# A second modulation in two halves, and seven smaller moves between VectorE, ScalarE and GpSimd, in a two-layer transformer kernel

## The chip, the cores and the metric

The kernel runs on one core of one Trainium2 chip, in one launch. The metric is the device time of one execution in microseconds (us). Three executions of the kernel before gave a median of 621.16 us (621.09 to 622.55).

A core has five engines that take part here. TensorE multiplies matrices and transposes, VectorE, ScalarE and GpSimd do elementwise work, and SyncE (SP) mostly issues DMA transfers. Each engine takes its instructions strictly in its own order. An instruction whose input is not there yet holds all that stand behind it on its engine.

## The reference, cut to what matters

Two layers run one after the other over `x` of 8 batches, 256 tokens and 128 features. In each layer a small vector `c` per batch is turned into six modulation vectors, which scale, shift and gate the two halves of the layer. The change touches layer 0 and the modulation of layer 1.

```python
mod = (silu(c) @ wmod).reshape(8, 6, 1, 128)       # once for each layer
sa, ca, ga, sb, cb, gb = mod[:, 0], ..., mod[:, 5]
ga = (2 * (ga >= 0) - 1) * maximum(abs(ga), 0.25)  # gb likewise
h = layernorm(x) * (1 + ca) + sa
x = x + ga * attention(h)
h = layernorm(x) * (1 + cb) + sb
x = x + gb * mixture(h)

# layer 0, attention: 16 heads of 8 features, causal
qkv = x @ W_qkv + b_qkv
scores = einsum('bhqd,bhkd->bhqk', q, k) / sqrt(8)  # then the causal mask
out = softmax(scores) @ v, heads put together
return out @ W_out + b_out
# layer 0, mixture: a shared network 128 -> 512 -> 128 (gelu), and of
# eight experts of the same size the two best of each token
probs = softmax(x @ Wr); topk_p, topk_i = top_k(probs, 2)
```

Layer 1 has 16 heads of 64 features and sixteen small experts, again two for each token.

## The kernel before, in words

**Two paths.** `fast_path` does all the work. It leaves out the subtraction of the maximum in the softmax, so it keeps a record of whether the row sums stayed in a safe range: `judge` (L798) folds reciprocals of row sums into a tile `good` with two VectorE steps (L801, L802). At the end a flag says whether `general_path` has to run as well. With these inputs it does not.

**The order of work.** The functions called in `fast_path` issue instructions at once, so the order of calls is the order in which each engine gets its instructions. A hand-written plan sets it. Lists `at`, `at_end` and `at_head` attach small steps to the passes of one loop, and the loop is this (L1421):

```python
for n in range(N0):          # N0 = 24 passes: 8 batches of 3 units
    b, u = divmod(n, 3)
    scores0(b, u, ...)       # 4 matmuls, 2 exps, masks; at_head steps inside
    if n == 0: set_up()
    if u == 1 and b + 1 < B: project0(b + 1)
    ...                      # the steps given by at(n, ...)
    if n > 1: values0(*divmod(n - 2, 3))
    if u == 1 and b + 1 < B: project_v0(b + 1)
    ...                      # the steps given by at_end(n, ...)
```

**A unit** is one pass. Units 0 and 1 of a batch take the first 128 keys for half of the heads each, unit 2 takes the last 128 keys and queries. `scores0` fills two score tiles `sc` in PSUM with two matmuls each (L1095), ScalarE takes an exp of 128x1024 from each into `pt` (L1099), and GpSimd clears what the causal mask forbids (L806). `values0` for the unit two passes back multiplies `pt` with the values into `o` (L1120). The values tile `vm` holds, for each head, 8 columns of values in a field of 32, with a column of ones at 16 or 17, which gives the row sum.

**Projections of a batch.** In the middle unit of a batch `project0` makes queries and keys of the next one: two matmuls `qk` (L1059), the key bias by one VectorE step (L1062), and four copies `qm` of the queries by ScalarE, each with the heads of one group kept and biased (L1064). `project_v0` comes at the end of the same unit: two matmuls `vp` and eight VectorE steps that add the value bias and place the columns into `vm` (L1081).

**After a batch.** At the end of the next batch's middle unit, `normalise0` (L1126) turns `o` around (`ot`), takes the reciprocals `r` of the row sums, scales (`at`) and turns back (`aT`). Two units later `finish0` (L1150) projects `aT` (`y`, L1156), scales by the gate `ga` and adds to `x`; `judge0` then tests the batch's reciprocals. The output bias, already multiplied by the gate, is added to `x` for two batches at a time by `add_bias`, a 128x512 addition on GpSimd (L1148).

**Norms.** `layernorm_parts` (L730) splits a norm into `measure` (statistics `st`, mean and variance `mv`), `normalise` (reciprocal root `rstd`, then `xn`, L756) and `modulate` (transposes `nt`, L765, and `h`, L768). For the tags listed in `by_power` the reciprocal root is made by two GpSimd steps at the end of `measure`: an addition (L745) and a power (L746). For all other norms ScalarE takes a root (L752) and VectorE a reciprocal (L753) in `normalise`. The first-half norms of layer 0 are `0a0` to `0a3`, for two batches each. The second-half norms are `0b0`, `0b2`, `0b4` for two batches and `0b6`, `0b7` for one. `0b2` and `0b4` are measured in units 15 and 21, `0b6` and `0b7` after the loop. [...] a change between the root, the exp (L1099, and L1200 in the router) and the gelu (L1233) loads a table.

**The router** of layer 0 (`route0`, L1185) follows each second-half norm: logits `lg`, an exp, the best two of eight, the slot of each token, and then one indirect DMA for each 128 tokens and choice (L910), which GpSimd issues and which writes the normalised tokens (`tokens`, two GpSimd steps) sorted by expert into DRAM. The steps are given out one at a time, over units 10 to 14 and the following heads, 16 to 20, and 22 to the end. After the loop (L1438 to L1492) come the last batches, the shared network (`shared_hidden0`, L1230), and a range test `judge0` of the last batch. Then 39 expert tiles of 128 tokens run (L1495): rows come by DMA, `turn0` transposes them (`xT`, `xTs`), `hidden0` and `tile_project0` apply the expert, a copy `ysb` of the result goes to DRAM. Copies `ysb` take two buffers in turn, those of the tags `aT` and `r`. Each buffer of a pool is reused only after its last reader is done.

**Modulation.** `modulation(n)` (L674) makes six projections `mp` on TensorE (L677; a matmul counts twice in the trace[...]) and moves them into `md[n]` with three VectorE steps (L681 to L683). `finish_modulation(n)` (L685) does twelve more tiny VectorE steps: one plus `cb`, the clamped gates, and the gated bias (L697). `rows_of(n, md)` (L699) transposes the result (`mr`, L702), copies it and sends it to DRAM, from where layer 1 will read it as rows. For layer 1 the three are called one behind the other at the end of unit 2, by `second_modulation`.

Of the kernel before, what the change touches and what calls it, by code (L numbers as in the profile page):

```python
# [16 lines left out]
P = 128  # L17
# [5 lines left out]
H = 16  # L23
# [534 lines left out]
def fast_path(ctx: ExitStack, tc: tile.TileContext, i: dict, out: bass.AP, bad: bass.AP):  # L558
# [62 lines left out]
    for base, cm, step in ((0, 1, -D0), (D0 - 1, -1, D0)):  # L621
# [1 line left out]
            out=hm, in_=hm, compare_op=ALU.is_ge, fill=0.0, base=base,  # L623
            pattern=[[step, H]], channel_multiplier=cm,
        )
    vm = [ap0.tile([P, 2, H, 32], F32, tag=f"vm{n}", bufs=1, name=f"vm{n}") for n in range(3)]

    def clear_vm(n):
        nc.gpsimd.memset(vm[n], 0.0)
        for m in range(2):  # L630
            nc.gpsimd.memset(vm[n].rearrange("p k (a m) c -> p (k a) m c", m=2)[:, :, m, 16 + m : 17 + m], 1.0)

    clear_vm(0)
    ints = const.tile([P, 65], I32, name="ints")
# [95 lines left out]
    def layernorm_parts(w, m, ks, kc, tag, ps_, tokens=None, tiles=range(TT)):  # L730

        kept = []
        nt = len(tiles)
        by_power = tag.startswith(('0a', '0b0', '1a0'))

        def measure():
            st = small.tile([P, nt, 6], F32, tag="st", name=f"st{tag}")
            mv = small.tile([P, nt, 2], F32, tag="mv", name=f"mv{tag}")
            for k, j in enumerate(tiles):
                nc.vector.bn_stats(st[:, k, :], x[w][:, j, :])  # L740
            for k in range(nt):
                nc.vector.bn_aggr(mv[:, k, :], st[:, k, :])
            rstd = small.tile([P, nt, 1], F32, tag="rstd", name=f"rstd{tag}")
            if by_power:
                nc.gpsimd.tensor_tensor(rstd, mv[:, :, 1:2], eps.unsqueeze(1).to_broadcast([P, nt, 1]), ALU.add)  # L745
                nc.gpsimd.tensor_tensor(rstd, rstd, minus_half.unsqueeze(1).to_broadcast([P, nt, 1]), ALU.pow)  # L746
            kept.extend((mv, rstd))

        def normalise():
            rstd, mv = kept.pop(), kept.pop()  # L750
            if not by_power:
                nc.scalar.activation(rstd, mv[:, :, 1:2], AF.Sqrt, bias=eps)  # L752
                nc.vector.reciprocal(rstd, rstd)  # L753
            xn = lnp.tile([P, nt, P], F32, tag="xn", name=f"xn{tag}")
            for k, j in enumerate(tiles):
                nc.vector.tensor_scalar(  # L756
                    xn[:, k, :], x[w][:, j, :], mv[:, k, 0:1], rstd[:, k, :], ALU.subtract, ALU.mult
                )
            kept.append(xn)

        def modulate():
            xn = kept[0]
            nt_ps = ps_([P, nt * P], f"nt{tag}")
            for k in range(nt):
                nc.tensor.transpose(nt_ps[:, bass.ts(k, P)], xn[:, k, :], ident)  # L765
            for k in range(nt * P // S):
                b = w * (TW // S) + tiles[0] * P // S + k
                nc.vector.tensor_scalar(  # L768
                    batch_cols(h, b), nt_ps[:, bass.ts(k, S)], m[:, kc, b : b + 1], m[:, ks, b : b + 1],
                    ALU.mult, ALU.add,  # L770
                )
            if tokens:
                tokens(w, xn)

        return [measure, normalise, modulate]
# [279 lines left out]
    def project0(b):  # L1055
        hb = batch_cols(h, b)
        qk = ps_ln([P, 2, S], f"qk0_{b}")
        for k in range(2):
            nc.tensor.matmul(out=qk[:, k, :], lhsT=wqkv[:, bass.ts(k, P)], rhs=hb, start=True, stop=True)  # L1059
        qm = ap0.tile([P, 4, S], F32, tag="qm", name=f"qm0_{b}")  # L1060
        k = ap0.tile([P, S], F32, tag="k", name=f"k0_{b}")
        nc.vector.tensor_scalar(k, qk[:, 1, :], bqkv[:, 1:2], None, ALU.add)  # L1062
        for j in range(4):
            nc.scalar.activation(  # L1064
                qm[:, j, :], qk[:, 0, :], AF.Identity, bias=jb[:, j : j + 1], scale=jm[:, j : j + 1]
            )
        st0["qk", b] = qm, k

    def project_v0(b):
        hb = batch_cols(h, b)  # L1070
        vp = ps_ln([P, 2, P], f"vp0_{b}")
# [4 lines left out]
        v = vm[b % 3].rearrange("p k (g j) m -> p (k g) j m", j=4)  # L1076
        vs = vp.rearrange("p k (g j d) -> p (k g) j d", j=4, d=D0)
        bs = bv.rearrange("p (g j d) -> p g j d", j=4, d=D0)
        for j in range(4):
            for n in range(2):  # L1080
                nc.vector.tensor_tensor(  # L1081
                    v[:, bass.ts(n, 4), j, bass.ts(j % 2, D0)], vs[:, bass.ts(n, 4), j, :], bs[:, :, j, :], ALU.add
                )

    def scores0(b, u, between):

# [22 lines left out]
    def values0(b, u):  # L1109
        v = vm[b % 3]  # L1110
        pt = st0.pop(("pt", b, u))
        if u == 0:
            st0["o", b] = pp.tile([P, 2, S], F32, tag="o", name=f"o0_{b}")
        o = st0["o", b]

        for n in range(2 if u < 2 else 4):
            j = 2 * u + n if u < 2 else n
            for g in range(4):
                q = bass.ds(0, S) if u < 2 else bass.ds(P, P)
                nc.tensor.matmul(  # L1120
                    out=o[bass.ts(g, 32), j // 2, q], lhsT=v[:, u // 2, 4 * g + j, :],
                    rhs=pt[:, g, bass.ts(n, S if u < 2 else P)],
                    start=(u == 0 and n == 0), stop=(u == 2 and n == 3), skip_group_check=True,
                )

    def normalise0(b):  # L1126

        o = st0.pop(("o", b))
        ot = ap0.tile([P, 2, S // 32, 32], F32, tag="ot", bufs=1, name=f"ot0_{b}")
        nc.vector.transpose(ot.rearrange("p s k c -> p (s k c)"), o.rearrange("p s q -> p (s q)"))  # L1130
        r = st0["r", b] = ap0.tile([P, 2, S // 32, 2], F32, tag="r", name=f"r0_{b}")
        nc.vector.reciprocal(r, ot[:, :, :, 16:18])
        at = ap0.tile([P, S // 32, 2, 2, D0], F32, tag="t", name=f"at0_{b}")
        for s in range(2):
            nc.vector.tensor_tensor(
                at[:, :, s], ot[:, s, :, 0:16].rearrange("p k (m d) -> p k m d", m=2),
                r[:, s].unsqueeze(3).to_broadcast([P, S // 32, 2, D0]), ALU.mult,
            )
        aT = ap0.tile([P, S], F32, tag="aT", name=f"aT0_{b}")
        nc.vector.transpose(aT, at.rearrange("p k s m d -> p (k s m d)"))  # L1140
        st0["aT", b] = aT

    def judge0(b):
        judge(st0.pop(("r", b)).rearrange("p s k m -> p (s k m)"))

    def add_bias(w):

        nc.gpsimd.tensor_tensor(by_batch(x[w]), by_batch(x[w]), of_batches(mdb0[:, BG - 1], w), ALU.add)  # L1148

    def finish0(b):  # L1150
        aT = st0.pop(("aT", b))
# [148 lines left out]
    def tile_project0(n):  # L1300
        hs, wt = tl.pop(("hs", n)), tl.pop(("w", n))
        y = pp.tile([P, P], F32, tag="o", name=f"yt_{n}")
        for c in range(FC):
            nc.tensor.matmul(  # L1304
                out=y, lhsT=hs[:, c, :], rhs=wt[:, bass.ds(WF + c * P, P)], start=(c == 0), stop=(c == FC - 1)
            )
        ysb = ap0.tile([P, P], F32, tag=("aT", "r")[n % 2], name=f"ysb_{n}")
        nc.vector.tensor_copy(ysb, y)  # L1308
        nc.sync.dma_start(out=z0.ys[bass.ts(n, P), :], in_=ysb)

# [36 lines left out]
        nc.gpsimd.memset(most, P - 0.5)  # L1347

    N0 = 3 * B
    at_head(2, 0, lambda: add_bias(0))  # L1350
    at_end(2, lambda: second_modulation())
    for w in range(1, NW):
        measure, normalise, modulate = layernorm_parts(w, md[0], SA, CA, f"0a{w}", ps_ln)
        n = 6 * w - 6
        at_end(n, measure)
        at(n + 1, normalise)
        at_end(n + 3, modulate)
        at_head(n + 2, 1, lambda w=w: add_bias(w))
    for b in range(B - 1):
        at_end(3 * b + 4, lambda b=b: normalise0(b))  # L1360
        if b < B - 2:
            at(3 * b + 6, lambda b=b: finish0(b))
            at_end(3 * b + 6, lambda b=b: judge0(b))
        else:
            at_end(3 * b + 5, lambda b=b: finish0(b), lambda b=b: judge0(b))
    ways = {}
    for bs in SPANS0[:3]:
        n = 3 * sum(bs) + 3
# [23 lines left out]
    z0 = Sorted(xp, "0", E0, NTT, (2 * NT - 2) // P)  # L1392
    z1 = Sorted(xp, "1", E1, 3 * TT, ND1)
    gates = ap0.tile([P, NTT, 32], F32, bufs=1, name="gates")
    wst = []

    def set_up():
# [15 lines left out]

    rd1 = []

    def second_modulation():
        modulation(1)
        finish_modulation(1)
        rd1.append(rows_of(1, md[1]))

    for n in range(N0):  # L1421
        b, u = divmod(n, 3)
        scores0(b, u, behind.pop(n, {}))
# [1 line left out]
            set_up()  # L1425
        if u == 1 and b + 1 < B:
            project0(b + 1)
        for step in early.pop(n, ()):
            step()
        if n > 1:  # L1430
            values0(*divmod(n - 2, 3))
        if u == 1 and b + 1 < B:
            project_v0(b + 1)
        for step in ends.pop(n, ()):
            step()

# [49 lines left out]
    for n in range(E0, E0 + 2):  # L1486
        fetch_weights0(n)
    one(shared_add0(1))()
    judge0(B - 1)
    turn_gates0(3)  # L1490
    shared_project0(2)
    tables()  # L1492
# [725 lines left out]
```

## Time and profile before

The lines that matter, from the profile of one execution:

| | |
|---|---|
| median of three executions | 621.16 us (621.09 to 622.55) |
| the profiled execution | 625.56 us; span 623.8 us, mean granted clock 0.940 |
| busy in the span: TensorE matmuls, weight loads | 548.0 us (88%), 388.9 us (62%) |
| VectorE, ScalarE, GpSimd | 352.9 us (57%), 275.8 us (44%), 292.0 us (47%) |
| chain of waits, by engine | TensorE 63%, VectorE 18%, DMA 8%, ScalarE 4% |
| layer 0's attention loop | from about 16 to 134 us |
| expert tiles of layer 0 | from 170 to 253 us, one every 1.89 us |
| layer 1 | from about 265 us |

The span runs from the first to the last instruction in the trace; the device time includes a little around it. All times within the execution are counted from the start of the span. "PE" is TensorE's matmul pipe and "PEld" its weight loads, "DVE" is VectorE, "ACT" ScalarE, "POOL" GpSimd. The page cuts the span into 40 slices of equal length and gives each engine's busy share in tenths for each slice, and for "PEclk" the clock that TensorE was granted. A wait is printed as the waiting instruction, an arrow, and the instruction that released it. An instruction is printed with its output, its inputs, the tiles' shapes and a count.

### The profile page before, as it was taken

To read this page: it belongs to the slowest core of one execution; us is meant where nothing else is said; L and a number is where in the kernel's file an instruction comes from. 1 tells how busy PE (TensorE), PEld (TensorE's weight loads), DVE (VectorE), ACT (ScalarE), POOL (GpSimd) and SP (SyncE) were. 2 spreads that over 40 slices of the span, in tenths; PEclk is the share of its full clock that TensorE was granted. 3 is DMA by queue.
4 is the path that set the end of the run, shared out by engine and by line. 5 is a ranking of instruction groups with operands and counts; after the bars stand their busy time and mean duration, and the time that the engine had idled before them with its cause. 6 is when DMAs were issued, how large, how long until landed. Compare 5 with 4: busy or idle time off the path is not lost.

```text
span 623.8 us, 11930 instructions
## 1 busy us (share of the span) xinstructions
PE 548.0 (88%) x4391; PEld 388.9 (62%) x4391; DVE 352.9 (57%) x1073; ACT 275.8 (44%) x487; POOL 292.0 (47%) x445
## 2 busy tenths in 40 slices
PE   5698979878799998789999999999999998988970
PEld 3344435445699998656676767667676766764450
DVE  5538896855732221246536556565838485644683
ACT  2566565545055554345534363345353532522430
POOL 5536686866314442238532056643445543104750
PEclk9989888879999998979999999999999999878986
DMA  7799991220329997131030203130303036563441
GB/s 271 281 399 407 393 362 52 65 90 30 108 71 325 316 333 231 35 151 35 19 86 6 64 18 88 30 73 2 78 14 82 18 74 187 165 176 76 105 104 57
DMA packets 53568, 85.41 MB, mean 137 GB/s; under 512 B 6653, under 2 KB 32765, under 8 KB 52349
## 3 DMA queue, kind: packets, MB, share of 16 engines
q1 hardware_dynamic: 45308, 60.50, 30.7%
q0 software_dynamic: 8048, 23.67, 12.3%
q8 instruction: 37, 0.61, 0.4%
q10 hardware_dynamic: 144, 0.39, 0.2%
q14 instruction: 31, 0.25, 0.1%
HBM read 53.46 MB, written 31.07 MB: 136 GB/s over the span
## 4 chain that ended last, share of the span: by engine, by line
PE 63%; DVE 18%; DMA 8%; ACT 4%; issue 3%; POOL 2%; SPq 1%; DVEq 0%; POOLq 0%; ACTq 0%
PE sc L1581 7%; PE o L1603 6%; PE qp L1550 5%; PE hp L1296 5%; PE vp L1563 5%; PE kp L1550 4%; PE yt L1304 4%; PE y L1656 4%; DMA wt<-in_wpk_dram,widx 3%; PE sc L1095 3%; PE sum L1611 3%; PE o L1120 2%; PE qk L1059 2%; PE hp L1230 1%; DMA gp<-gd 1%
## 5 line engine op out<-in xcount | busy, mean ns | idle before, releaser
L806 POOL TENSOR_SCALAR_AFFINE_SELECT pt<-pt 128x256 f32<-128x256 f32 (+1 forms) x176 | 89.4, 533 | 112.1 <-ACT pt L1584 79.8
L1033 POOL DMA_INDIRECT yg<-ys,yidx x56 | 54.1, 966 | 52.8 <-DMA ys<-ysb 34.5
L1584 ACT ACTIVATE pt<-sc 128x768 f32<-128x768 f32 x64 | 48.5, 808 | 25.6 <-PE sc L1581 25.4
L1099 ACT ACTIVATE pt<-sc 128x1024 f32<-128x1024 f32 x48 | 46.5, 1021 | 24.0 <-PE sc L1095 23.0
L1025 POOL DMA_INDIRECT wt<-in_wpk_dram,widx x31 | 29.1, 938 | 52.8 <-PE xT L1287 51.1
L1298 ACT ACTIVATE hst<-hp,wt 128x128 f32<-128x128 f32 x136 | 38.9, 368 | 32.9 <-ACT hst L1298 18.8
L1581 PEld LDWEIGHTS sc<-q,k 64*128 64x128 f32 x512 | 41.5, 187 | 16.5 <-issue 11.5
L1581 PE MATMUL sc<-q,k 64*128 64x256 f32 (+1 forms) x512 | 50.5, 336 | 0.0
L1603 PE MATMUL o<-pt,v 128*64 128x256 f32 (+1 forms) x512 | 48.7, 332 | 1.8 <-POOL pt L806 1.8
L1566 ACT COPY v<-vp 128x512 f32<-128x512 f32 x32 | 18.8, 586 | 67.9 <-PE vp L1563 57.1
L1308 DVE COPY ysb<-yt 128x128 f32<-128x128 f32 x39 | 11.4, 292 | 60.6 <-PE yt L1304 60.6
L1603 PEld LDWEIGHTS o<-pt,v 128*64 128x64 f32 x512 | 31.9, 136 | 19.7 <-POOL pt L806 5.6
L1554 DVE COPY q<-qp 128x512 f32<-128x512 f32 x32 | 22.0, 688 | 39.0 <-PE qp L1550 39.0
L1095 PE MATMUL sc<-qm,k 32*128 32x512 f32 x192 | 37.7, 738 | 3.4 <-ACT pt L1099 2.7
L1296 PE MATMUL hp<-xTs,wt 128*128 128x128 f32 x272 | 37.4, 281 | 3.7 <-DMA wt<-in_wpk_dram,widx 2.7
L1550 PE MATMUL qp<-h,wq 128*128 128x256 f32 x128 | 37.0, 412 | 1.3 <-DVE sh L1257 1.3
L910 POOL DMA_INDIRECT xs<-ht0b,idx x32 | 31.7, 990 | 13.4 <-issue 4.8
L1563 PE MATMUL vp<-wv,h 128*128 128x512 f32 x64 | 36.4, 652 | 1.1 <-DVE q L1554 1.1
L1296 PEld LDWEIGHTS hp<-xTs,wt 128*128 128x128 f32 x272 | 33.8, 195 | 5.5 <-issue 3.3
L1304 PE MATMUL yt<-wt,hst 128*128 128x128 f32 x272 | 36.6, 279 | 0.0
L1554 ACT COPY k<-kp 128x512 f32<-128x512 f32 x32 | 18.8, 588 | 35.4 <-PE kp L1550 35.4
L1304 PEld LDWEIGHTS yt<-wt,hst 128*128 128x128 f32 x272 | 33.9, 196 | 0.0
(289 smaller groups left out, 1129.8 us busy)
## 6 DMA issues: line engine op xcount, KB each, us to landing
xs<-zero SPq DMA_DIRECT2D x1, 12288.0 KB
xs<-zero SPq DMA_DIRECT2D x1, 8192.0 KB
rb<-rd SPq DMA_DIRECT2D x14, 512.0 KB
mdb<-mrd SPq DMA_DIRECT2D x2, 2048.0 KB
xg<-xs SPq DMA_DIRECT2D x63, 64.0 KB
wt<-in_wpk_dram SPq DMA_DIRECT2D x24, 128.0 KB
wst<-in_wpk_dram SPq DMA_DIRECT2D x5, 514.0 KB
ys<-ysb SPq DMA_DIRECT2D x10, 256.0 KB
```

What stands on the lines that cost most here:

```text
L806: nc.gpsimd.affine_select(out=pt, in_=pt, compare_op=ALU.is_ge, fill=0.0, base=0, pattern=[[0, pt.shape[1]], [1, P]], channel_multiplier=-1,)
L1033: nc.gpsimd.indirect_dma_start(out=yg[:, k, :], out_offset=None, in_=self.ys[:, :], in_offset=bass.IndirectOffsetOnAxis(ap=self.yidx[:, j, ...
L1095: nc.tensor.matmul(out=sc[:, n, :].rearrange("p (a q) -> p a q", q=rhs.shape[2]), lhsT=k[r, cols], rhs=rhs, start=True, stop=True,)
L1099: nc.scalar.activation(pt[:, bass.ts(half, 2), :], sc, AF.Exp)
L1296: nc.tensor.matmul(out=hp[:, c, :], lhsT=wt[:, bass.ts(c, P)], rhs=xT, start=True, stop=True)
L1304: nc.tensor.matmul(out=y, lhsT=hs[:, c, :], rhs=wt[:, bass.ds(WF + c * P, P)], start=(c == 0), stop=(c == FC - 1))
L1550: nc.tensor.matmul(out=ps_[:, n, :], lhsT=w1[f"w{what}1"][:, bass.ts(2 * u + n, P)], rhs=hb, start=True, stop=True)
L1554: copy(st1[what, b, u], ps_)
L1563: nc.tensor.matmul(out=vp, lhsT=hb[:, bass.ts(j, P)], rhs=w1["wv1"][:, bass.ts(half, 512)], start=True, stop=True)
L1581: nc.tensor.matmul(out=sc[:, n, cols], lhsT=k[r, m, bass.ts(kb, P)], rhs=q[r, m, qs], start=True, stop=True)
L1584: nc.scalar.activation(pt, sc[:, :, 0:384], AF.Exp, scale=1.0 / math.sqrt(D1))
L1603: nc.tensor.matmul(out=o[bass.ts(n, D1), m, qs], lhsT=v[:, kb, bass.ts(4 * (u % 2) + 2 * m + n, D1)], rhs=pts[m][:, n, cols], start=(kb == ...
```

## The change

Seven things are changed.

- The three parts of the second modulation are called at three places: the projections at the end of unit 3, the small VectorE steps at the end of unit 4, the transposition and its DMA at the end of unit 7.
- All norms of layer 0 take the reciprocal root by GpSimd's power; no ScalarE root is left in layer 0.
- The key bias is added by ScalarE, ahead of the four query steps, not by VectorE.
- The value bias of a batch is one VectorE step. For that, the ones of `vm` lie at columns 16 and 41 of a field of 64 for each pair of heads, and the odd head's window of 32 columns begins at 24.
- The bias on `x` is added by VectorE, at the ends of units 3, 8, 14 and 20; before, GpSimd did it at heads of units 2, 2, 8 and 14.
- The reciprocals of all batches are kept in one tile `rs0` and tested once, ahead of the expert tiles, by two steps over 256 elements a partition.
- `project_v0` is called right behind `project0`.

As a consequence `r` is no tag of the pool any more, and the copies `ysb` take the tags `aT`, with two buffers, and `ot`, with one.

```diff
-    vm = [ap0.tile([P, 2, H, 32], F32, ...) for n in range(3)]
+    vm = [ap0.tile([P, 2, H // 2, 64], F32, ...) for n in range(3)]
...
-            nc.gpsimd.memset(vm[n]...[:, :, m, 16 + m : 17 + m], 1.0)
+            nc.gpsimd.memset(vm[n]...[:, :, 16 + 25 * m : 17 + 25 * m], 1.0)
...
-        by_power = tag.startswith(('0a', '0b0', '1a0'))
+        by_power = tag.startswith(('0', '1a0'))
...
-        nc.vector.tensor_scalar(k, qk[:, 1, :], bqkv[:, 1:2], None, ALU.add)
+        nc.scalar.activation(k, qk[:, 1, :], AF.Identity, bias=bqkv[:, 1:2])
...
-        for j in range(4):
-            for n in range(2):
-                nc.vector.tensor_tensor(
-                    v[:, bass.ts(n, 4), j, bass.ts(j % 2, D0)], vs[:, bass.ts(n, 4), j, :], bs[:, :, j, :], ALU.add
-                )
+        nc.vector.tensor_tensor(
+            vm[b % 3].rearrange("p k a (m c) -> p k (a m) c", m=2)[:, :, :, 0:D0],
+            vp.rearrange("p k (h d) -> p k h d", d=D0),
+            bv.rearrange("p (h d) -> p h d", d=D0).unsqueeze(1).to_broadcast([P, 2, H, D0]), ALU.add,
+        )
...
-                    out=o[bass.ts(g, 32), j // 2, q], lhsT=v[:, u // 2, 4 * g + j, :],
+                    out=o[bass.ts(g, 32), j // 2, q], lhsT=v[:, u // 2, 2 * g + j // 2, bass.ds(24 * (j % 2), 32)],
...
-        r = st0["r", b] = ap0.tile([P, 2, S // 32, 2], F32, tag="r", name=f"r0_{b}")
+        r = rs0[:, b]
...
-    def judge0(b):
-        judge(st0.pop(("r", b)).rearrange("p s k m -> p (s k m)"))
...
-        nc.gpsimd.tensor_tensor(by_batch(x[w]), by_batch(x[w]), of_batches(mdb0[:, BG - 1], w), ALU.add)
+        nc.vector.tensor_tensor(by_batch(x[w]), by_batch(x[w]), of_batches(mdb0[:, BG - 1], w), ALU.add)
...
-        ysb = ap0.tile([P, P], F32, tag=("aT", "r")[n % 2], name=f"ysb_{n}")
+        tag, bufs = (("aT", 2), ("ot", 1))[n % 2]
+        ysb = ap0.tile([P, P], F32, tag=tag, bufs=bufs, name=f"ysb_{n}")
...
-    at_head(2, 0, lambda: add_bias(0))
-    at_end(2, lambda: second_modulation())
+    at_end(3, lambda: add_bias(0), lambda: modulation(1))
+    at_end(4, lambda: finish_modulation(1))
+    at_end(7, lambda: rd1.append(rows_of(1, md[1])))
...
-        at_head(n + 2, 1, lambda w=w: add_bias(w))
+        at_end(n + 8, lambda w=w: add_bias(w))
...
-            at_end(3 * b + 6, lambda b=b: judge0(b))
...
-            at_end(3 * b + 5, lambda b=b: finish0(b), lambda b=b: judge0(b))
+            at_end(3 * b + 5, lambda b=b: finish0(b))
...
+    rs0 = ap0.tile([P, B, 2, S // 32, 2], F32, bufs=1, name="rs0")
...
             project0(b + 1)
+            project_v0(b + 1)
...
-        if u == 1 and b + 1 < B:
-            project_v0(b + 1)
...
-    judge0(B - 1)
+    judge(rs0.rearrange("p b s k m -> p (b s k m)"))
```

More of the change, by code (lines that the diff above doesn't have):

```diff
@@ L625, in fast_path @@
         )
-    vm = [ap0.tile([P, 2, H, 32], F32, tag=f"vm{n}", bufs=1, name=f"vm{n}") for n in range(3)]
+    vm = [ap0.tile([P, 2, H // 2, 64], F32, tag=f"vm{n}", bufs=1, name=f"vm{n}") for n in range(3)]
     def clear_vm(n):
@@ L630, in clear_vm @@
         for m in range(2):
-            nc.gpsimd.memset(vm[n].rearrange("p k (a m) c -> p (k a) m c", m=2)[:, :, m, 16 + m : 17 + m], 1.0)
+            nc.gpsimd.memset(vm[n].rearrange("p k a c -> p (k a) c")[:, :, 16 + 25 * m : 17 + 25 * m], 1.0)
     clear_vm(0)
@@ L1075, in project_v0 @@
             )
-        v = vm[b % 3].rearrange("p k (g j) m -> p (k g) j m", j=4)
-        vs = vp.rearrange("p k (g j d) -> p (k g) j d", j=4, d=D0)
-        bs = bv.rearrange("p (g j d) -> p g j d", j=4, d=D0)
-        for j in range(4):
-            for n in range(2):
-                nc.vector.tensor_tensor(
-                    v[:, bass.ts(n, 4), j, bass.ts(j % 2, D0)], vs[:, bass.ts(n, 4), j, :], bs[:, :, j, :], ALU.add
-                )
+        nc.vector.tensor_tensor(
[3 more added lines that the diff above has]
+        )
     def scores0(b, u, between):
@@ L1414, in fast_path @@
     rd1 = []
[L1416 to L1419, printed above, removed]
     for n in range(N0):
```

## The prediction

> **What bounds the kernel now.** I read the page's slices, then TensorE's waits inside the attention loop of layer 0, then the chain, then timelines of the spots these name. The slices (15.6 us each) place the edits: all but the `ysb` buffers lie in the first eleven, and layer 1, from about 265 us, runs the same instructions as before.
>
> ```profile
> PE   5698979878799998789999999999999998988970
> DVE  5538896855732221246536556565838485644683
> POOL 5536686866314442238532056643445543104750
> PEclk9989888879999998979999999999999999878986
> ```
>
> TensorE is nearly full from slice 10 on. In slices 1 to 9 it has gaps, and VectorE and GpSimd stand at 8 and 9 there. No engine is full alone: they hand a wait to each other. The waits of TensorE from 22 to 134 us (total us, times, longest):
>
> ```profile
> PE mr L702 <- DVE md L697: 5.2, 1, 5.2
> PE nt0b L765 <- DVE xn0b L756: 4.2, 4, 2.5
> PE qk L1059 <- DVE h L768: 3.9, 2, 3.6
> PE sc L1095 <- ACT pt L1099: 1.8, 5, 1.2
> PE y L1156 <- DVE aT L1140: 1.3, 2, 0.8
> ```
>
> The first is the second modulation: its transposition `mr` stands in TensorE's queue behind fifteen small VectorE steps, and everything after it waits. The chain of waits shows the same (start, us, what):
>
> ```profile
> 25.45 1.45 PE mp L677 x12
> ...
> 31.84 0.15 DVE md L697
> ...
> 32.13 0.38 PE mr L702
> 32.51 2.02 PE sc L1095 x8
> 34.53 1.86 PE o L1120 x16
> ```
>
> The same eight score matmuls take 1.07 us at 37.21 and sixteen value matmuls 1.00 at 24.45, so the wait also costs half speed afterwards. The third view is unit 21 to 22 (a unit is one pass of the loop, a third of a batch), where a norm of the second half of layer 0 runs:
>
> ```profile
> 115.97 0.35 DVE L742 BATCH_NORM_AGGREGATE mv0b<-st0b 128x2 f32<-128x6 f32 x4
> 116.36 0.30 ACT L752 ACTIVATE rstd0b<-mv0b,eps 128x4 f32<-128x4 f32 x1 [1.48 <-DVE mv0b L742]
> 117.07 1.35 DVE L756 TENSOR_SCALAR xn0b<-x,mv0b,rstd0b 128x128 f32<-128x128 f32 x4
> ```
>
> ```profile
> 116.92 0.64 POOL L806 TENSOR_SCALAR_AFFINE_SELECT pt<-pt 128x512 f32<-128x512 f32 x1
> 117.73 1.02 POOL L910 DMA_INDIRECT xs<-ht0b,idx  x1 [0.17 <-issue]
> 119.08 0.62 POOL L806 TENSOR_SCALAR_AFFINE_SELECT pt<-pt 128x512 f32<-128x512 f32 x1 [0.32 <-ACT pt L1099]
> ```
>
> The root comes 0.4 us after the variance from ScalarE, while GpSimd, working without a gap since 105.83, is still on the masks and scatters of unit 21 until 118.75.
>
> [...] the 128x4 add at L1214 takes 2.97 us at 82.71, over a mask and the x bias on GpSimd, and 0.15 at 158.72. [...]
>
> **The change part by part.**
>
> *Second modulation split.* The 5.2 us wait goes: the six projections `mp` (x12) stay on TensorE (1.45 us) at the end of unit 3, `mr` (0.38) at the end of unit 7 finds them long done. Score matmuls of unit 3 then wait only for exps that end by 27, so they start at about 26 instead of 32.44; with 2.4 us of scores and values, 1.5 of `mp`, 0.7 of transposes and 1.1 of scores, unit 4's projection comes at 31.7 instead of 38.22: **-6.5** (bounds -5.2, the bare wait, to -7.0, with all of the half speed). Of the fifteen steps three go behind unit 3 and twelve behind unit 4, some 1.7 us together at full speed (14.39 to 16.07 for the first modulation); VectorE is busy 6.2 of 13 us in 35 to 48. The first `normalise0` is queued behind them and had 1.3 us of slack, so up to 0.6 may return. The DMA of `mr` changes nothing: SP is held by the expert weights until 86 in both, and its data is wanted at about 260.
>
> *Keys by ScalarE.* VectorE loses 0.48 us a batch (L1062) and the queries no longer wait for it; ScalarE gains 0.48 (four query steps take 1.93 at 40.21). Queued behind them is the next exp, and a score tile waits for that. Where ScalarE ran without a pause (40, 50, 77, 107 us) this costs 0.48 each. I charge the first two, **+1.0**; the others fall where GpSimd ends last, below. Bounds 0 to +2. The first batch changes by under 0.1.
>
> *Value bias in one step, judged once, x bias on VectorE.* Eight steps of 0.11 pitch (0.88) become one of 0.42: -0.46 a batch. Two range steps, 0.4 a batch, leave the loop seven times; the eighth pair grows from 0.38 to 0.85 (L801 and L802 have 424 ns rows at 256 elements) and stands before `xTs` of the first expert tile, for which TensorE waits 2.4 us at 167.9 to 170.3: **+0.5**. The x bias adds 0.69 (the L1260 row, same shape) four times to VectorE and takes 1.275 four times from GpSimd. Together VectorE loses 1.3 us a batch, less 0.69 every second one. Of this, much is hidden: at 48 and 59 the key and range steps sit inside the wait for GpSimd's power (49.83 and 60.32).
>
> *Values right behind queries.* At unit 10 the projection (0.71) fills the 0.68 us in which TensorE waits for `xn0b`; at unit 16 `lg` no longer waits 1.0 for the value bias.
>
> *Norms by power.* Four norms (batches 2-3, 4-5, 6, 7) leave ScalarE: four Sqrt, seven table loads of 1.28. They cost GpSimd 0.2 + 1.03 us each, 1.42 from variance to `xn` (58.94 to 60.36) if it is free, against 0.63 now. It is not free: in the built order the power stands behind all masks and scatters of its unit. In units 13 to 16 that stream is gapless from 76.06 and its last scatter ends at 90.41; without the x bias at 84.38 (1.27 + 0.17) at 89.0, so `xn` starts at 90.3 where it started at 90.70. In units 19 to 21 it ends at 118.75 and nothing shortens it: power 118.8 to 120.05, started 0.3 earlier, `xn` at 119.8 instead of 117.07: **+2.7**. For batch 6 it waits for the `seen` steps (to 130.88): `xn` at 132.2 instead of 131.01, **+1.2**, and the slot indices, so the scatters, are behind it on VectorE. For batch 7 it stands behind those scatters and their tokens: **+0.9**. The loads themselves free the exps at 86.2 and 115.2, where TensorE waits for VectorE anyway: nothing.
>
> *Expert tiles.* Odd `ysb` has one buffer for two. A tile takes 1.89 us, so a buffer is wanted again after 3.79; copy 0.3 and DMA 1.52 (the last one on the chain) make 1.8. Under the weight gathers it isn't shown; bounds 1.8 and the gathers' 4.9 to 6.9 us landing, which move eight times as much. I take nothing.
>
> **Sum by stretch.** To unit 6: -6.5 + 0.5. Units 7 to 9: -0.3 (value bias ahead of `aT`) + 0.5. Units 10 to 12: -1.2 (`lg` 0.9 sooner, exp of the router 1.2). Units 13 to 18: `h` for the query projection at 85.9 instead of 89.86, but `nt0b` then waits for the power until 90.7; `lg` and unit 17 follow 2.7 sooner, 2.1 after the router: -2.1. Units 19 to 21: 0. From unit 22: +2.7 - 0.4 (range steps) + 1.2 + 0.9. Tables: +0.5. Total **-4.2 us**. The profiled execution is 625.56 (span 623.8 and 1.8 around it), 4.4 above the median of 621.16; on the median the sum gives **617.0**. A measurement can tell about 0.3%, 1.9 us.
>
> **The rivals.** *A: GpSimd isn't late* (0.2). Its stream starts earlier by what VectorE saves, the powers cost little, and -6.5, -1.2 and some 4 in units 13 to 18 stay: -10, 611. For it: 25 us of VectorE's own waits. Against: the gapless stream. *B: the gain is eaten* (0.15): keys charged in all four batches (+2) and each moved x bias blocked once by a mask (1.1 us, as the 1.85 us pair at 53.44): -1, 620. *C: slower* (0.13): GpSimd becomes the bound. The powers sit ahead of the masks of the next unit too, for which the values wait; if each of the three late ones holds TensorE 4 us instead of 1.6, plus half speed of 1.5 each after it, the tail costs 7.2 + 4.5 more, +7.5, 628.7; it decides from 4.2 us of extra loss on. For it: the power of unit 21 comes 3 us after its input. Against: TensorE never waits over 0.6 for a mask now. That the modulation split does nothing is excluded: TensorE waits in order for it. A slow landing of `ysb` above 3.7 us (0.02) would go the same way.
>
> **The numbers.** Forecast 0.5, 617.0, its own range 613 to 620. With A the range reaches 611, with B and part of C 622. Faster by over 0.3% (under 619.3): 0.68; within: 0.17; slower: 0.15.
>
> **What would show it.** Right: no wait of `mr`; `sc` of unit 3 near 26; ScalarE without loads between 16 and 130; GpSimd powers at L746 for 0b2, 0b4 starting 2 to 4 us after their `mv`, and `nt0b` of unit 22 with a wait near 5 us. Wrong: powers on time (A), exps waiting after queries in every batch (B), masks that hold `o` (C), or `ysb` copies waiting for DMA.

## The result, and the profile after

The changed kernel took 628.05 us at the median of 20 executions (620.55 to 636.06); the kernel before took 622.12 (619.49 to 623.12, 20 executions). The ratio is 1.0062, with a 95% interval of 1.0037 to 1.0087: slower by 0.6%, where 617.0 and a range of 611 to 622 had been forecast. (The ratio leaves out the seven longest runs of the changed kernel, from 630.63 us up, so it is below that of the two medians, 1.0095; the profiled execution, with 630.86 us and a span of 629.1, is one of the seven.)

The two profiled executions are 5.3 us apart. What a part of the change is worth in the totals is taken from the experiments.

The starts of eight pieces of work on TensorE show where the time went. They are read from the timelines, in us from the start of the span; the last column is the difference between the two profiled executions.

| start of | before | after | difference |
|---|---|---|---|
| projection `qk` in unit 4 | 38.22 | 31.88 | -6.3 |
| scores of unit 10 | 58.05 | 51.28 | -6.8 |
| scores of unit 16 | 85.07 | 75.26 | -9.8 |
| scores of unit 22 | 114.02 | 105.49 | -8.5 |
| scores of unit 23 | 122.52 | 117.50 | -5.0 |
| `nt0b` of batch 7 | 145.51 | 141.31 | -4.2 |
| first expert tile | 170.30 | 168.86 | -1.4 |
| shared network of the last tokens (end of the tiles) | 252.97 | 259.71 | +6.7 |

So there are three acts: a gain of up to 9.8 us in the attention loop, most of it given back from unit 22 to the first expert tile, and a loss of 8.2 us in the expert tiles (82.7 us before, 90.9 after). Behind the tiles nothing is added: 369.4 us to the end of the span, 370.8 before.

The slices of the page after are 15.7 us each. The second act begins in slices 7 and 8 (94 to 126 us), where TensorE is busy 7 and 7 tenths (before: 9 and 8), VectorE 5 and 5 (before: 6 and 8), while GpSimd is at 8 in the first of them (before: 6), and where the granted clock falls to 6 tenths in the second (before: 8). The third lies in slices 14 to 16 (204 to 252 us), with TensorE at 8, 8 and 7 (before: 9, 9 and 8):

```profile
PE   5998777788699887969999999999999998888970
DVE  4277965554632121146644657466647576745683
POOL 5447868575214432337551154742355644104750
PEclk9999979678799998979999999999999998989997
```

TensorE's waits from 22 to 134 us (total us, times, longest), where `mr` led the list before:

```profile
PE nt0b L765 <- DVE xn0b L756: 7.2, 3, 5.5
PE sc L1092 <- ACT pt L1096: 4.0, 7, 0.7
PE nt0b L765 <- DVE vm L1076: 4.0, 2, 2.9
PE qk L1059 <- DVE h L768: 3.1, 1, 3.1
```

The wait of `mr` is gone; the transposes `nt0b` of the second-half norms have taken its place. Two of their waits, 1.0 us in unit 10 and 2.9 in unit 16, end with the value bias `vm`, which stands ahead of them since `project_v0` follows `project0`. No run takes that move back, so what it is worth stays open. The chain of waits around unit 3 (start, us, what) now has the scores at 25.91 where it had them at 32.51, and nothing of the modulation but its projections:

```profile
25.91 2.04 PE sc L1092 x8
...
28.95 1.44 PE mp L677 x12
```

In the timeline of unit 21 to 22, GpSimd takes the power (L745, L746) only after the masks and scatters of the unit, 3.5 us after VectorE has the variance, and `nt0b` waits 5.5 us:

```profile
106.25 0.36 DVE L742 BATCH_NORM_AGGREGATE mv0b<-st0b 128x2 f32<-128x6 f32 x4
109.05 0.97 POOL L910 DMA_INDIRECT xs<-ht0b,idx  x1 [0.17 <-issue]
110.05 0.21 POOL L745 TENSOR_TENSOR rstd0b<-mv0b,eps 128x4 f32<-128x4 f32 x1
110.34 1.04 POOL L746 TENSOR_TENSOR rstd0b<-rstd0b,minus_half 128x4 f32<-128x4 f32 x1
111.41 1.84 DVE L756 TENSOR_SCALAR xn0b<-x,mv0b,rstd0b 128x128 f32<-128x128 f32 x4 [4.81 <-POOL rstd0b L746]
112.12 0.99 PE L765 MATMUL nt0b<-ident,xn0b 128*128 128x128 f32 x3 [5.50 <-DVE xn0b L756]
```

The third act is read from the line of the copies `ysb` (L1308, now L1303) and what VectorE sat idle for ahead of them (us, times). In the kernel before, all 39 copies waited only for TensorE's `yt`:

```profile
L1308 DVE COPY ysb<-yt x39: 291/292/293, 174.8 to 253.2; 128x128 f32<-128x128 f32 x39
...
  PE yt L1304: 60.6, 39
```

In the changed kernel:

```profile
L1303 DVE COPY ysb<-yt x39: 278/291/293, 173.9 to 259.9; 128x128 f32<-128x128 f32 x39
...
  DMA ys<-ysb: 39.2, 10
  PE yt L1298: 27.0, 17
```

Ten copies wait for the earlier transfer out of their buffer, 39.2 us in all, and the timeline of VectorE shows the rhythm:

```profile
205.58 0.29 DVE L1303 COPY ysb<-yt 128x128 f32<-128x128 f32 x1 [3.57 <-DMA ys<-ysb]
205.99 0.28 DVE L1303 COPY ysb<-yt 128x128 f32<-128x128 f32 x1
210.43 0.29 DVE L1303 COPY ysb<-yt 128x128 f32<-128x128 f32 x1 [3.97 <-DMA ys<-ysb]
210.84 0.28 DVE L1303 COPY ysb<-yt 128x128 f32<-128x128 f32 x1
```

One copy of a pair waits, the other follows at once, and this pair of tiles takes 4.85 us, not twice 1.89 (the eight pairs from 201 to 240 us take 4.5 to 5.2, the next one 7.4). SyncE's queue issues the first of these transfers at 205.90. The trace gives the landing of a `ys` transfer in this stretch:

```profile
DMA to landing us min/median/max: 3.7/4.4/4.5
```

Copy 0.3, issue, 4.4 to land, then the next copy: that is the 4.85. Where the trace gives a landing before the weight gathers (178 to 182 us) and after them (from 257), it is 1.5.

### The profile page after: what moved, and what is told of

The parts are those of the page before. It is cut to its first block, busy times and chain, and to the rows that moved or that the text cites. A ratio compares the mean times of both kernels' runs of the same rounds, so it can differ in the third digit from the quotient of the medians.

```text
span 629.1 us, 11843 instructions
## 1 busy us (share of the span) xinstructions
PE 543.6 (86%) x4391; PEld 385.9 (61%) x4391; DVE 339.3 (54%) x995; ACT 267.7 (43%) x484; POOL 292.4 (46%) x449
## 4 chain that ended last, share of the span: by engine, by line
PE 57%; DVE 15%; DMA 11%; ACT 7%; POOL 5%; issue 3%; SPq 0%; DVEq 0%; POOLq 0%; ACTq 0%
DMA ys<-ysb 8%; PE sc L1571 7%; PE o L1593 6%; PE qp L1540 5%; PE y L1646 5%; PE vp L1553 5%; PE kp L1540 4%; PE sum L1601 3%; PE hp L1290 3%; PE yt L1298 3%; PE sc L1092 2%; PE hp L1224 2%; ACT pt L1096 2%; POOL xs L910 2%; ACT qm L1064 1%
## 5 line engine op out<-in xcount | busy, mean ns | idle before, releaser
L1303 DVE COPY ysb<-yt 128x128 f32<-128x128 f32 x39 | 11.3, 289 | 70.0 <-DMA ys<-ysb 39.2
L1092 PE MATMUL sc<-qm,k 32*128 32x512 f32 x192 | 37.4, 702 | 5.5 <-ACT pt L1096 4.8
L1290 PEld LDWEIGHTS hp<-xTs,wt 128*128 128x128 f32 x272 | 33.8, 195 | 13.2 <-DVE xTs L1283 12.7
L910 POOL DMA_INDIRECT xs<-ht0b,idx x32 | 32.0, 1000 | 15.5 <-DVE redg L1209 5.2
```

The lines of the kernel that those rows point to most:

```text
L910: self.apart(nc.gpsimd.indirect_dma_start(out=self.xs[:, :], out_offset=bass.IndirectOffsetOnAxis(ap=idx[:, j, k : k + 1], axis=0), in_=to ...
L1092: nc.tensor.matmul(out=sc[:, n, :].rearrange("p (a q) -> p a q", q=rhs.shape[2]), lhsT=k[r, cols], rhs=rhs, start=True, stop=True,)
L1290: nc.tensor.matmul(out=hp[:, c, :], lhsT=wt[:, bass.ts(c, P)], rhs=xT, start=True, stop=True)
```

## The experiments

The twelve kernels ran in three sittings, in which the kernel before took 642.1, 621.3 and 641.5 us at the median. So each is compared by its ratio to the kernel before of the same sitting, and one percent of it is about 6.2 us. The first four ran in the first sitting, the next four in the second, the last four in the third. All but e2_ysb_alone and e4_mod_alone were changed from a kernel that was measured in an earlier sitting, and then the difference of two ratios takes for granted that the sittings differ by a common factor, which no run shows. The stages come from one profile of each kernel.

### Three buffers in turn

```diff
-        tag, bufs = (("aT", 2), ("ot", 1))[n % 2]
+        tag, bufs = (("aT", 2), ("aT", 2), ("ot", 1))[n % 3]
```

> The changed kernel with its three ysb buffers used in turn (tile n waits for the DMA of tile n-3 instead of n-2 for odd n). Theory 1 (the loss is made in the expert tiles by the single buffer of the odd copies): the copy no longer waits, the tiles go back to a pitch of 1.89 us, the stretch from the first expert tile to the shared network of the last tokens is 83 us instead of 90.9, and the kernel takes 620 to 621, 1 to 2 us under the kernel before, with the small spread of the kernel before. Theory 2 (the transfers themselves have become slower, and any buffer would wait): the stretch stays over 88 us, the time near 627. Theory 3 (the loss is in layer 1 or in the attention loop): no difference from the changed kernel, 628.

Measured: ratio 0.9964 (0.9942 to 0.9986). The tiles' stretch is 79.7 us (167.83 to 247.50). The copies have one releaser again:

```profile
  PE yt L1298: 57.9, 39
```

The same three buffers, each reused after three tiles, let no copy wait: 3 x 1.89 = 5.7 us is more than the loop of 4.85. In all profiles whose copies don't wait for a transfer the tiles take 79.3 to 82.7 us, so the long stretch comes from the single odd buffer. It made the whole loss, 0.98 points (6 us), and the rest of the change is a gain of about 2 us.

### The buffers alone

```diff
-        ysb = ap0.tile([P, P], F32, tag=("aT", "r")[n % 2], name=f"ysb_{n}")
+        tag, bufs = (("aT", 2), ("ot", 1))[n % 2]
+        ysb = ap0.tile([P, P], F32, tag=tag, bufs=bufs, name=f"ysb_{n}")
```

This is the kernel before with that one edit. There the tags `aT` and `r` have two buffers each, so a buffer comes back after four tiles, 7.6 us.

> The kernel before with the ysb buffers of the changed one (aT two, ot one) and nothing else changed. Theory 1: the tiles' stretch grows from 82.7 to about 90 us, the total to 628 to 630, with a spread of several us. Theory 2: ysb lands faster here than in the changed kernel, no wait, 622. Theory 3: 622.

Measured: ratio 1.0147 (1.0108 to 1.0187), about 9 us. Eight of its copies wait 27.0 us for the transfer. Its tiles took 86.5 us, less than the 90 expected, but the profiled execution is the shortest of the six. The loss doesn't need the rest of the change.

### Two buffers

```diff
-        tag, bufs = (("aT", 2), ("ot", 1))[n % 2]
-        ysb = ap0.tile([P, P], F32, tag=tag, bufs=bufs, name=f"ysb_{n}")
+        if "yb" not in tl:
+            tl["yb"] = ap0.tile([P, 2, P], F32, tag="ot", bufs=1, name="ysb_two")
+        ysb = tl["yb"][:, n % 2]
```

> The changed kernel with two ysb buffers in all (even and odd copies one each). Theory 1, with the loop copy, issue, landing, next copy as the bound of a pair of tiles: the even copies now wait too, but in the same loop of some 4.85 us a pair, so the stretch stays 90 to 94 us and the total 628 to 631. A rival in which each buffer that is waited for adds its own wait to every tile: 98 us or more, total over 635.

Measured: ratio 1.0072 (1.0040 to 1.0104) against the changed kernel's 1.0062; the tiles take 89.4 us (167.77 to 257.17), both a little under what was expected. With one buffer fewer no further loss shows, so the bound is the loop of one buffer, not the number of waits: 16 copies wait here, 35.5 us in all. Kernel e1_turn3, 1.1 points lower, ran in the same sitting.

### The modulation split alone

```diff
-    at_end(2, lambda: second_modulation())
+    at_end(3, lambda: modulation(1))
+    at_end(4, lambda: finish_modulation(1))
+    at_end(7, lambda: rd1.append(rows_of(1, md[1])))
```

> The kernel before with the second modulation split alone. By the prediction's step: unit 4 starts its projection 6.5 us sooner, and with nothing later to take it back the total is 5 to 6.5 us lower, 616 to 617. The rival, that later waits for VectorE and GpSimd take it up (as the changed kernel's first expert tile, only 1.4 us earlier, would allow): 619 to 621.

Measured: ratio 0.9933 (0.9908 to 0.9957), 4.2 us. Unit 4's projection comes at 32.05, as in the changed kernel, but unit 7 at 43.73, not at 40.75. TensorE's longest wait from 22 to 66 us in this kernel, and the scores behind it in the timeline, show what took three microseconds back:

```profile
PE y L1156 <- DVE aT L1140: 1.6, 1, 1.6
```

```profile
43.73 2.09 PE L1095 MATMUL sc<-qm,k 32*128 32x512 f32 x8
```

VectorE, now with the modulation's small steps in the same units, has `aT` late, and the scores after the wait run at half speed: 2.09 against 1.14 in the changed kernel, where the granted clock is 1.00 from 43 to 46 us. The slow stretch begins right behind the wait of 1.6 us (39.1 to 40.7): `y` takes 1.22 at 40.71, in the changed kernel 0.71 at 39.11.

### Roots by ScalarE again

```diff
-        by_power = tag.startswith(('0', '1a0'))
+        by_power = tag.startswith(('0a', '0b0', '1a0'))
```

This and the next three start from e1_turn3.

> e1_turn3 with the four norms 0b2, 0b4, 0b6, 0b7 by ScalarE's root again, as in the kernel before. By the prediction's step (late powers cost 2.7 + 1.2 + 0.9, table loads cost nothing): nt0b of unit 22 comes 5 us after the score tile's start less 3, the shared network 4 to 5 us sooner than in e1_turn3, and the total 3 to 5 us under it (ratio to before near 0.990). Rival: the scatters of GpSimd and their tokens end the stretch ahead of the expert tiles anyway, or the seven table loads take it back: within 1 us of e1_turn3.

Measured: ratio 0.9830 (0.9797 to 0.9862), 10.6 us under the kernel before and 1.3 points under e1_turn3, about 8 us where 3 to 5 were expected. The two kernels of the same sitting that keep all powers stand at 0.9985 and 0.9992 (e7_keys_vector, e8_bias_gpsimd). The timeline at the same place:

```profile
104.84 0.36 DVE L742 BATCH_NORM_AGGREGATE mv0b<-st0b 128x2 f32<-128x6 f32 x4
105.24 0.30 ACT L752 ACTIVATE rstd0b<-mv0b,eps 128x4 f32<-128x4 f32 x1 [0.44 <-DVE mv0b L742]
105.55 1.28 ACT L1096 ACT_TABLE_LOAD   x1
105.78 2.04 DVE L756 TENSOR_SCALAR xn0b<-x,mv0b,rstd0b 128x128 f32<-128x128 f32 x4
```

`xn0b` starts 1.85 us after the scores of unit 22 (103.93) where the power in the changed kernel let it start 5.9 after them. Unit 23 starts at 112.05 (e1_turn3: 117.47), `nt0b` of batch 7 at 132.79 (140.96), the first expert tile at 160.89 (167.83). Table loads are back (at this place two, at 103.51 and 105.55, of 1.28 us each), and no wait of TensorE for them shows here.

### Only the three late norms by ScalarE

```diff
-        by_power = tag.startswith(('0', '1a0'))
+        by_power = tag.startswith(('0a', '0b0', '0b2', '1a0'))
```

> As e5_sqrt, but norm 0b2 stays with GpSimd's power. If the late powers are the three from unit 21 on, as the prediction says, unit 17 starts as in e1_turn3 (89.2) and the rest gains as in e5_sqrt: 3 to 4.5 us under e1_turn3. If 0b2 is late as well (nt0b of unit 16 comes 9 us after the scores there, 6.7 in the kernel before), e5_sqrt beats this by about 1 us.

Measured: ratio 0.9836 (0.9801 to 0.9871), the same as e5_sqrt. Unit 17 follows unit 16 by 12.7 us, in e5_sqrt by 11.7; but e10_scatters_later and e1_turn3, alike there and both with this power, have 11.8 and 13.8. TensorE's speed differs there: the values of unit 14 behind `nt0b` take 1.08 us in the first and 1.93 in the second, the scores of unit 17 1.14 and 2.09. So what the power of 0b2 costs at that place stays open. The first tile starts at 160.82, as in e5_sqrt, but that is in part chance: at `nt0b` of batch 7 e5_sqrt is 2.7 us ahead (132.79, 135.49), and its third shared layer gives 1.7 back (5.40 us for 3.70). In the totals no price of 0b2 shows, to some 3 us; the gain that shows is that of the three late ones.

### Keys on VectorE

```diff
-        nc.scalar.activation(k, qk[:, 1, :], AF.Identity, bias=bqkv[:, 1:2])
+        nc.vector.tensor_scalar(k, qk[:, 1, :], bqkv[:, 1:2], None, ALU.add)
```

> e1_turn3 with the key bias back on VectorE. By the prediction's step (keys by ScalarE cost 0.48 in two batches): 1 us sooner at unit 10, and at most that in the total. Rival: VectorE's 0.48 a batch delays normalise0 and the value bias as it did before, and the loop is later by up to 2 us at unit 22, which the wait for GpSimd's power there absorbs: no difference in the total.

Measured: ratio 0.9985 (0.9966 to 1.0005). From the first scores (14.67, in e1_turn3 14.35) it takes 37.6 us to unit 10 and 92.2 to unit 22, in e1_turn3 37.1 and 91.9. So a cost of 1 us of the keys on ScalarE is not there. The 0.3 to 0.5 us the other way is too little to call a gain: e1_turn3, e3_two and e10_scatters_later, alike up to unit 10, take 37.0 to 37.4 to it. The totals' intervals overlap.

### The x bias on GpSimd

```diff
-        nc.vector.tensor_tensor(by_batch(x[w]), ...)
+        nc.gpsimd.tensor_tensor(by_batch(x[w]), ...)
...
-    at_end(3, lambda: add_bias(0), lambda: modulation(1))
+    at_head(2, 0, lambda: add_bias(0))
+    at_end(3, lambda: modulation(1))
...
-        at_end(n + 8, lambda w=w: add_bias(w))
+        at_head(n + 2, 1, lambda w=w: add_bias(w))
```

> e1_turn3 with the x bias on GpSimd at its old places. By the prediction's step, GpSimd's stream in units 13 to 16 is longer by 1.4 us and its power for 0b2 that much later, unit 17 1 to 1.5 us later; the late power of unit 21 isn't changed by it (its x bias lies ahead). Total 0 to 2 us over e1_turn3. Rival: VectorE's 0.69 a step[...] is the greater cost, and the total falls by 1 us.

Measured: ratio 0.9992 (0.9970 to 1.0014). Unit 17 starts at 90.55 against 89.24, 1.3 us later, as expected, though that place moves by as much between kernels that are alike there. In the changed kernel three of the four additions on VectorE take 0.68 to 0.69 us and the one at 47.36, while GpSimd works on masks, 1.37. The total stands 0.3 points over e1_turn3, which the intervals don't tell apart. The first tile comes 3.1 us later (170.91, 167.83). Of that 2.4 stand at `nt0b` of batch 7 (143.35, 140.96); then the third shared layer takes 5.40 for 3.70, and about 1 us is made up ahead of the copy `gT`.

### The value bias in eight steps

From e5_sqrt; the same sum, in the new layout:

```diff
-        nc.vector.tensor_tensor(... one step over [P, 2, H, D0] ...)
+        for j in range(4):
+            for n in range(2):
+                nc.vector.tensor_tensor(
+                    v[:, bass.ts(n, 4), j // 2, j % 2, 0:D0], vs[:, bass.ts(n, 4), j, :], bs[:, :, j, :], ALU.add
+                )
```

> e5_sqrt with the value bias in eight VectorE steps again (in the new layout of the values tile), at the new place behind the queries. By the prediction's step (0.46 a batch, much of it hidden, some 0.3 taken in units 7 to 9): score tiles of unit 10 at most 0.5 us later than in e5_sqrt (51.3), total 0 to 1 us over it. Rival: the shorter step is what lets aT be ready in time once the modulation's small steps stand in units 3 and 4 (in e4_mod_alone y waits 1.6 us for it there and half speed follows): unit 7 starts 2 to 3 us later than in e5_sqrt (40.8), total 2 to 4 us over it.

Measured: ratio 0.9877 (0.9842 to 0.9912), against 0.9830. Unit 7 starts 2.0 us later than in e5_sqrt (42.80, 40.75), unit 10 2.3 later (53.55, 51.28), the first tile 3.2. In this kernel TensorE's waits from 24 to 66 us have the line that e4_mod_alone had, smaller:

```profile
PE y L1153 <- DVE aT L1140: 0.8, 1, 0.8
```

The stages favour the rival. The one-step bias is worth 2 to 3 us by them, since it makes room on VectorE where the split puts the modulation's steps. The totals, 0.5 points apart, agree but would not show it alone.

### Two scatters behind the power

From e1_turn3, norm 0b4 by power:

```diff
             for k in range(7):
-                at_head(n + 4 + k // 2, k % 2, go)
+                m = 2 * (n + 4) + k
+                if bs[0] == 2 and k > 3:
+                    m += 2
+                at_head(m // 2, m % 2, go)
```

> e1_turn3 with the two scatters of unit 21 moved two heads on, into units 22 and 23, so that GpSimd reaches the power of norm 0b4 without them. If the price of a power is its place in GpSimd's queue: the power starts some 2 us sooner than 110.1, unit 23 starts 2 us sooner than 117.5, and the total is 1 to 2 us under e1_turn3 (ratio to before near 0.994). If it is the power itself, or what follows it on VectorE: no change at unit 23.

Measured: ratio 0.9951 (0.9930 to 0.9971) against 0.9964. GpSimd's timeline, the scores of unit 22 having started at 104.52:

```profile
106.63 0.20 POOL L745 TENSOR_TENSOR rstd0b<-mv0b,eps 128x4 f32<-128x4 f32 x1
106.91 1.04 POOL L746 TENSOR_TENSOR rstd0b<-rstd0b,minus_half 128x4 f32<-128x4 f32 x1
```

The power's two steps start 1.35 us after the variance does (105.28), in e1_turn3 3.8 (107.08, 110.88). Units 22 and 23 are 9.4 us apart, in e1_turn3 11.3, in e5_sqrt 8.1. Two scatters moved give back 1.9 us of 3.2, so most of the price is the power's place in the queue. In the total it is 0.1 points, in the expected direction and below what can be told; the two scatters have to be issued later all the same.

### The best of these, with the range test moved

From e6_sqrt_late:

```diff
     shared_hidden0(2)
+    judge(rs0.rearrange("p b s k m -> p (b s k m)"))
     go7()
...
     one(shared_add0(1))()
-    judge(rs0.rearrange("p b s k m -> p (b s k m)"))
```

> e6_sqrt_late with the range test moved from ahead of the first expert tile to the end of the third shared hidden layer, where VectorE waits over 4 us for the router's ranks. The 0.85 us leave the path to the first tile: 0.5 to 0.9 us under e6_sqrt_late, ratio to before 0.981 to 0.983. Rival: the ranks' wait isn't idle time to spare, and the scatters come later: the same or worse than e6_sqrt_late.

Measured: ratio 0.9854 (0.9817 to 0.9892), not told apart from e6_sqrt_late. VectorE's timeline shows that the two steps lie inside the wait for the ranks:

```profile
143.84 0.42 DVE L801 SCALAR_TENSOR_TENSOR good<-rs,good 128x256 f32<-128x256 f32 x1
144.30 0.42 DVE L802 SCALAR_TENSOR_TENSOR good<-rs,good 128x256 f32<-128x256 f32 x1
146.60 0.17 DVE L899 TENSOR_TENSOR at<-rk,region 128x16 f32<-128x16 f32 x1 [1.88 <-PE rk L897]
```

From the copy `gT` (152.24) to the first tile (161.64) it takes 9.4 us; in e6_sqrt_late 10.2 (150.64 to 160.82). So the 0.8 us are saved there. They don't show in the total. That copy itself waits 1.9 us, as in the three kernels beside it and in e1_turn3, where it waits 0.9 in the four of the second sitting; the cause of that is open.

### No split

From e5_sqrt, the modulation in one piece at the end of unit 2:

```diff
-    at_end(3, lambda: add_bias(0), lambda: modulation(1))
-    at_end(4, lambda: finish_modulation(1))
-    at_end(7, lambda: rd1.append(rows_of(1, md[1])))
+    at_end(3, lambda: add_bias(0))
+    at_end(2, lambda: modulation(1), lambda: finish_modulation(1), lambda: rd1.append(rows_of(1, md[1])))
```

> e5_sqrt with the second modulation in one piece at the end of unit 2, as in the kernel before. By the prediction's step the wait of mr and the half speed after it come back: unit 4 starts its projection 5.2 to 6.5 us later than in e5_sqrt (31.9), total 5 to 6.5 us over it, ratio to before near 0.992. Rival: as e4_mod_alone showed, part of the gain is taken back by later waits: 4.3 us or less.

Measured: ratio 0.9888 (0.9854 to 0.9922). The wait is back, though shorter than before:

```profile
PE mr L702 <- DVE md L697: 2.8, 1, 2.8
```

In the kernel before three of the small steps, beside the x bias, a mask and the x bias again on GpSimd, took 1.27, 0.92 and 1.25 us (L682, L687, L693); here, with the x bias on VectorE behind them, they take 0.61, 0.17 and 0.17. Unit 4's projection starts 4.9 us later than in e5_sqrt (36.78, 31.87), the first tile 6.4 (167.32, 160.89). The total is 0.58 points over, 3.6 us, with about 3 us of uncertainty: in company, too, the split is worth some 4 us, by the stages up to 6.

## Why the prediction was wrong

**The step that failed is "Expert tiles ... I take nothing".** It measured +8.2 us in the two profiles and about 6 in the totals (the changed kernel against e1_turn3). The prediction had the slack right, 3.79 us for a buffer wanted two tiles later. It priced the transfer by the last one of the stage, 1.52 us, which runs when the weight gathers have ended; under them it takes 3.7 to 4.8. The other bound, the gathers' own 4.9 to 6.9, was written down and would have decided the other way, but it was neither kept for the range nor given more than 0.02. With a loop of 4.85 for 3.79 the loss is 1.06 a pair. The 29 gathers go with about as many tiles, some fourteen pairs, so by this estimate up to 15 us belonged into the range. The one row not shown was put at its cheap end.

**Up to the first tile the sum held in part, and partly by luck.** Forecast: -4.2. Measured: -1.4 in the changed kernel's profile, -2.5 in that of e1_turn3, whose total is 2.2 us under the kernel before and would have lain in the range (0.9964 x 622.1 = 619.9). The signs named for being right came: no wait of `mr`, `sc` of unit 3 at 25.91, no table load in the loop, `nt0b` of unit 22 with a wait of 5.5. Of those for being wrong one came, copies `ysb` waiting for DMA.

- *Split:* -6.5 forecast, -6.3 at unit 4. That it was "excluded" to do nothing held. Its working overlooked what the moved steps do to `aT` when VectorE has no room: alone it is worth 4.2 (e4_mod_alone).
- *Value bias:* mis-sized. "-0.3 in units 7 to 9" measured 2.3 at unit 10, once the split is in (e9_eight_steps).
- *Keys:* the +1.0 isn't there; the loop without the move is 0.3 to 0.5 slower, about the difference of like kernels (e7_keys_vector).
- *Units 10 to 18:* by unit 19 a gain of 9.1 was forecast, by the sum, and 8.7 measured (104.23 to 95.54). The agreement is luck: units 10 to 12 gained 2.6 where 1.2 was forecast, and units 13 to 18 lost 0.7 where a gain of 2.1 was.
- *Late powers:* forecast +2.7 at unit 22; measured 2.9 (scores of unit 22 -8.5, `nt0b` -5.6, from 117.71 to 112.12). To batch 7 the forecast was +4.4, measured +4.3. This step was right against the kernel before. What undoing it brings is more, 6.9 us at the first tile: 2.3 of it stand at unit 22 already, 3.2 come between units 22 and 23, where `xn0b` with the root comes 1.2 us nearer to the scores than it did before, and 1.5 behind.
- *Tables:* +0.5 forecast, +2.8 measured from batch 7 to the first tile. The longer range test is the 0.5 that was forecast (0.85 for its two steps, 0.38 before). Another 1.7 is the third shared layer at 5.40 us where the same matmuls of e1_turn3 take 3.70: the granted clock was 0.50 from 149 to 152 us, in e1_turn3 1.00 from 135 to 150 and 0.92 in the mean of 150 to 172. The late powers don't decide that, for e5_sqrt has 5.40 without them.
- *A line misread:* the add of 0.15 us at 158.72 that is set against the 128x4 one of 2.97 has a tile of 128x2. One of 128x4 takes 0.16 at 156.84, with GpSimd idle, so the comparison stands; why the other took 2.97 isn't shown.

**The rivals.** A (GpSimd in time) fell: the additions ahead of the powers started 2.0 us (0b2) and 3.8 us (0b4) after their variance began. Of B's two costs, the keys show none, and the x bias on VectorE makes no difference that the totals can tell (e8_bias_gpsimd). C named the right side and, for the powers, part of the right cost, but not the mechanism that decided; without the odd buffer the kernel is faster than before.

## What to carry to other kernels

A ring of buffers is free only while (reuse distance) x (pitch) exceeds copy, issue and landing (here 3 x 1.89 us did and 2 x 1.89 did not exceed 4.85), with the landing taken under the traffic of that stage, not at its end; where the trace doesn't show it, both answers belong in the range. If it is short, change the order in which the buffers are used before asking for more memory. A step moved to an idle-looking engine costs what stands ahead of it in that engine's queue (here the power of 0b4 started 3.8 us after its variance, and 1.35 after it with two scatters moved behind it), so look at the queue at that moment, not at the share of the span. Edits that make room and edits that use it should be priced together: here the split alone lost 3 us to a late `aT`, which a shorter value bias on the same engine prevented.

## What the runs showed of the hardware

In the changed kernel a transfer of 64 KB out of SBUF landed in 1.5 us before and after the indirect weight gathers and in 3.7 to 4.8 beside them, where the DMA moved 293 GB/s (186 to 240 us); one issued at 247.6, when few gathers were left, landed in 2.9. In the kernel before TensorE's granted clock was 1.00 from 25 to 30 us and 0.51 from 30.0 to 30.5, within the wait of 5.25 us for `mr` (26.88 to 32.13). In e4_mod_alone the `y` and `o` behind a wait of 1.6 us took 1.22 and 1.94 us, in the changed kernel 0.71 and 1.07. TensorE kept the order of its queue: in the kernel before the scores of unit 3, whose last exp had ended at 26.90, started at 32.44, behind `mr` at 32.13; in the changed kernel, with `mr` moved, at 25.91. The changed kernel's 20 executions spread over 15.5 us, those of the kernel before over 3.6; that the loop over one buffer makes the spread isn't shown, since the six of e2_ysb_alone, with the same loop, spread over 4.6.
